# Large fp32 products as four column tiles, and a planner that knows the array's tilings

## The chip, the cores and the metric

The kernel runs on one core of one Trainium2 chip. The metric is the device time of one execution in microseconds (us), and lower is better. The core has five engines that work side by side and meet at semaphores: TensorE (PE, with its weight loads shown apart as PEld), VectorE (DVE), ScalarE (ACT), GpSimd (POOL) and SyncE (SP), which issues most of the transfers here.

## What is computed

Eight sequences of 512 tokens with 256 channels (x) pass through two layers; each has an attention part and a feed-forward part, and each part is added to x through a tanh gate. Everything is in fp32, apart from the quantised feed-forward products.

```python
x = x + tanh(g_xattn[0]) * L0_xattn(layernorm(x), ctx)   # 16 heads of 16: causal self + cross attention, one output projection
x = x + tanh(g_ffn[0])   * L0_ffn(layernorm(x))          # 8-bit affine quantised 256 -> 1024 -> gelu -> 256
x = x + tanh(g_xattn[1]) * L1_xattn(layernorm(x), ctx)   # two blocks, below
x = x + tanh(g_ffn[1])   * L1_ffn(layernorm(x))          # ternary weights 256 -> 1024, conv of 3 tokens, silu, -> 256

# one block of L1_xattn: 16 heads of 32, then an MLP; a1 attends to x, a2 to ctx (128 channels)
q, k, v = ln(x) @ wq, ln(y) @ wk, ln(y) @ wv
a = softmax(q @ k.T * 32 ** -0.5)        # in block a1 a strict mask follows the softmax
x_out = x + (a @ v) @ li1 + li1_b
out = x_out + gelu(ln(x_out) @ li2 + li2_b) @ li3 + li3_b    # 256 -> 1024 -> 256
```

## The kernel before

**Stages.** The work runs in four overlapping stages. By the trace, layer 0's attention lasts until about 713 us, layer 0's feed-forward part until about 1060 us, layer 1 with both its blocks and most of its feed-forward part until about 2600 us, and the rest is the end of the last sequences.

**Three tilings of the array.** The array of TensorE is used in three ways, which the trace shows in the form of each product:

- "rows" (`32*128`): the scores of attention, `ps_s<-QT,KT`. Four heads lie at partitions 0, 32, 64 and 96, and the four products of a set go to four row tiles (`front`, L1422 and L2206).
- "columns" (`128*32`): attention's product with the values, `ov<-pt,v`, `ov<-pt,vt` and `ov<-dg,vt`, and the sums of the exponentials, `ps<-acc,ones` and `ps<-pt,ones`. The four products of a set write to PSUM partitions 0, 32, 64 and 96 (`back`, L1441 and L2229).
- "whole" (`128*128`): all projections and MLP products in fp32 (`proj`, L1058, and direct calls of `mm`, L1052), the bf16 products of the feed-forward parts, the transposes (`tp`, L1056), and small products of 1 or 128 columns (`gains1`, `row_of`).

An fp32 product of any tiling appears in the trace as two MATMUL records and two LDWEIGHTS records; a bf16 product or a transpose as one of each. Nearly all go through `mm`, so the profile gives L1053 as their line, and they are told apart by their tiles: `ps<-x3T,li` and `ps<-li,hD` are the two MLP products of layer 1, `ps<-li,oT` its output projection, `ps<-zT,a_wq`, `ps<-zT,a_wk` and `ps<-a_wv,zT` its queries, keys and values; `xnT`, `ctxT` and `yT` belong to layer 0; `ps<-hp,diag` is a convolution done as products with diagonal matrices, in the tail of the last sequence only; `fw` and `f_w_q` are the bf16 weights of the feed-forward parts.

**Attention.** One step is a front and a back. A front writes four score products into two PSUM tiles (`ps_s`, tag `st`), and ACT takes their exponentials to `pt` (L1431, L2217); for masked blocks POOL clears part of it (L1434) or copies the masked diagonal to `dg` (L2221). The back multiplies with the values into `ov`, a PSUM tile of which there is one (tags `ov` and `ov1`). In layer 1, DVE adds the `pt` tiles of a group of four heads (`acc`, L2246 and L2248); the last back of a group forms the sums with `ones`, and then DVE turns them (`rt`, L2261), takes reciprocals, turns them back (`rb`, L2264) and multiplies them into `oT` (L2266), which frees `ov`. There are 64 groups in layer 1.

**What sets the order.** The order of instructions on every engine is fixed while the program is written. Two loops, `weave_timed` (L1067, layer 0) and `weave_all` (L1824, layer 1), choose again and again between the next step of attention and a number of generators ("streams") for projections, norms, the MLP and the feed-forward parts. A stream yields the tiles that its next piece needs. Of the pieces that could start by TensorE's planned time plus 0.3 us, the one with the lowest progress (base + share x work done / total) is written; if there is none, the one that can start first. `sooner` (L797) picks ACT or DVE for an evacuation by the planned times of both.

The planned times come from `Pace` (L756). Its `note` (L801) is called for every instruction and adds up when each engine is free (`free`), when each tile is ready (`done`) and last used (`used`), and how much work TensorE did (`work`). A tiled product is priced in `quarter` (L860), which keeps four lanes, one for each tile of the array; other products in `cost` (L874). A product's result counts as ready at the end of its streaming. `Pace.note` also ties each engine's instructions into the order in which they were written.

**Weights of the feed-forward parts.** `few_weights` (L1896) loads the bf16 weights of one feed-forward part from DRAM through SP (L1900) each time that a stream asks for them: `first(b)` (L1918) w2 of layer 0, `last(b)` (L2286) w1 and w2 of layer 1. The tiles `fw1` and `fw2` have one buffer each, and both layers use `fw2`. The streams run one after another: first 0 to 5, last 0, first 6, last 1, last 2, first 7, last 3 to 6. The tail of sequence 7 uses the weights that last 6 took.

Of the kernel before, what the change touches and what calls it, by code (L numbers as in the profile page):

```python
# [8 lines left out]
F32 = mybir.dt.float32  # L9
BF16 = mybir.dt.bfloat16  # L10
# [3 lines left out]
PSUM = bass.MemoryType.PSUM  # L14

P = 128
# [4 lines left out]
FF = 1024  # L21
# [7 lines left out]
FIRST_AT = (-1, 0, 1, 2, 4, 5, 7, 9)  # L29
LAST_AT = (6, 7, 8, 11, 12, 13, 15)  # L30
PTS = 3
KEYS_FIRST = 6


# [23 lines left out]
class General:  # L58
    def __init__(self, tc, ins, out):
        self.tc, self.nc, self.ins, self.out = tc, tc.nc, ins, out  # L60
# [695 lines left out]
class Pace:  # L756
# [2 lines left out]

    SIGNAL, OVERLAP = 0.04, 0.07

    def __init__(self, tc):
        self.tc, self.nc = tc, tc.nc
        self.free = {}
        self.done = {}
        self.used = {}
        self.rings = {}
        self.last = {}  # L770
        self.work = 0.0
        self.table = None
        self.wire = 0.0

        self.groups, self.lanes, self.start = None, [0.0] * 4, 0.0

    def open(self):
        self.nc.push_inst_callback(self.note)
# [22 lines left out]
    def note(self, ins):  # L801
        e = str(ins.engine).rsplit(".", 1)[-1]
        outs = [a.bass_ap for a in ins.outs if hasattr(a, "bass_ap")]
        srcs = [a.bass_ap for a in ins.ins if hasattr(a, "bass_ap")]
        if not outs or not srcs and ins.opcode != "Memset":
            return
        if e in self.last:
            self.tc.add_manual_dep(
                ins, self.last[e],
                mybir.DependencyInfo(mybir.DependencyClass.NoSync, mybir.DependencyReason.DATA),  # L810
                reason="woven order",
            )
        self.last[e] = ins.name
        out = self.name(outs[0])
        tiled = e == "PE" and 32 in tuple(ins.tile_size)
        t0 = 0.0 if tiled else self.free.get(e, 0.0)
        if out not in self.used:
            tile_ = outs[0].tensor
            bufs = getattr(tile_, "tag_meta", None) and tile_.tag_meta.bufs
            if bufs:  # L820
                tag = tile_.tag.rsplit("_", 2)[0]
                tiles, _, _ = ring = self.rings.get(tag, ([], 0, None))
                if ring[2] != tile_.owner_uid:
                    tiles, _, _ = self.rings[tag] = ([], bufs, tile_.owner_uid)
                if len(tiles) >= bufs:
                    t0 = max(t0, self.used[tiles[-bufs]] + self.SIGNAL)
                tiles.append(out)
        elif e != "PE" and ins.opcode != "DMACopy":
            t0 = max(t0, self.used[out] + self.SIGNAL)
        for a in srcs:  # L830
            t0 = max(t0, self.done.get(self.name(a), 0.0) + self.SIGNAL)
        if ins.opcode == "DMACopy":
            self.free[e] = t0 + 0.4
            n = 4 if outs[0].dtype == F32 else 2
            for _, k in outs[0].ap:
                n *= k
            self.wire = max(self.wire, t0 + 1.2) + n / 280e3
            end = self.wire + 1.2
        elif tiled:
            cost, end = self.quarter(ins, t0, outs)  # L840
        else:
            cost = self.cost(e, ins, outs, srcs)
            self.groups = None if e == "PE" else self.groups
            end = t0 + cost
            self.free[e] = end - (self.OVERLAP if e in ("DVE", "Activation") else 0.0)
            if e == "PE":
                self.work += cost
        self.done[out] = max(end, self.done.get(out, 0.0))
        for a in outs + srcs:
            n = self.name(a)  # L850
            self.used[n] = max(end, self.used.get(n, 0.0))
# [5 lines left out]
            n *= k  # L857
        return n

    def quarter(self, ins, t0, outs):  # L860

        rows = ins.tile_size[0] == 32
        if self.groups is not rows:
            self.groups, self.lanes = rows, [self.free.get("PE", 0.0)] * 4
        k = ins.tile_position[0 if rows else 1] // 32
        t = max(t0, self.lanes[k], self.start + 0.02)
        n = self.size(outs[0])
        cost = 0.19 + n * 0.0017 if rows else 0.1 + n * 0.00177
        self.start, self.lanes[k] = t, t + cost
        self.free["PE"] = max(self.lanes)  # L870
        self.work += cost / 4
        return cost / 4, t + cost

    def cost(self, e, ins, outs, srcs):  # L874
        size = self.size

        op = str(ins.opcode)
        n = max(size(a) for a in outs + (srcs if "Reduce" in op else []))

        few = sum(size(a) == 1 for a in srcs)  # L880
        if e == "PE":
            start = 0.0 if self.groups is None else 0.19
            if ins.is_transpose:
                return start + 0.095
            return start + max(0.22, n * 0.00169) if srcs[0].dtype == F32 else start + n * 0.00042
        if e == "Activation":
            f = str(getattr(ins, "func", "Copy")).rsplit(".", 1)[-1]
            sbuf = srcs[0].tensor.space != PSUM
            t = n * 0.00084 + 0.16
            if f == "Identity":  # L890
                t += 0.22 if sbuf else 0.09 * few
            elif f == "Gelu" and n <= T:
                t += 0.19
            if f in ("Exp", "Gelu", "Silu") and f != self.table:
                self.table = f
                t += 1.28
            return t
        psum = any(a.tensor.space == PSUM for a in outs + srcs)
        two = sum(size(a) == n for a in srcs) > 1
        if e == "Pool":  # L900
            if "Affine" in op:
                return 0.25 + n * 0.001
            return 1.05 if n <= 2 * NT and two else 0.22 + n * 0.0021
        if "Reduce" in op:
            return 0.14 + n * (0.00173 if len(srcs[0].ap) > 2 and list(srcs[0].ap)[-1][0] > 1 else 0.00106)
        if "BNStats" == op:
            return 0.41
        if n <= 4 * NT:
            return 0.17
        if psum or two or "Transpose" in op:  # L910
            return 0.15 + 0.05 * few + n * 0.00106
        return 0.15 + 0.05 * few + n * 0.0006
# [39 lines left out]
class Fast(General):  # L952
# [97 lines left out]


    def mm(self, out, lhsT, rhs, start=True, stop=True):  # L1052
        self.nc.tensor.matmul(out, lhsT, rhs, start=start, stop=stop, skip_group_check=True)  # L1053

    def tp(self, out, in_):
# [540 lines left out]
    def layer0_ffn(self):  # L1596
        nc, tc, small = self.nc, self.tc, self.small
        with (
# [15 lines left out]
            for b in range(B):  # L1614
                streams.append(Stream(self.range0(b), 4.7, 1.0, b))
            streams.append(Stream(self.chain(*(self.keys2(b) for b in range(KEYS_FIRST))), 64.0, B))
            self.weave_timed([], streams)
# [85 lines left out]
    def keys2(self, b):  # L1703

        work, w = self.work, self.w1s[1]
        cT = self.cTs.pop(0)
        if b + 2 < KEYS_FIRST:
            self.load_cT(b + 2)
# [5 lines left out]
    def keys2_rest(self):  # L1714
# [13 lines left out]

        load(KEYS_FIRST)
        load(KEYS_FIRST + 1)  # L1730
        for b in range(KEYS_FIRST, B):
            k = work.tile([P, 4, T], F32, tag="pt", name="k2", bufs=PTS)
            yield from self.keys_of(b, cTs[b], w[0], k)
            v = work.tile([P, NT, 2 * C], F32, tag="pt", name="v2", bufs=PTS)
            yield from self.values_of(b, cTs.pop(b), w[1], v)
# [31 lines left out]
    def layer1_xattn(self):  # L1767
        nc, tc = self.nc, self.tc
        with (
# [11 lines left out]
            self.hps = [wpool.tile([P, T // 2 + 3], F32, name=f"hp{i}") for i in range(2)]  # L1781
            for t in self.hps:
                nc.gpsimd.memset(t, 0.0)
            self.wl = {}


            self.pairs = self.fronts = self.backs = self.zTs = self.nvt = 0
# [26 lines left out]
            self.keys_done, self.x0_read = False, 0  # L1814
            keys = [Stream(self.keys2_rest(), 8.0 * (B - KEYS_FIRST), 1.0, -1.0)]
            self.weave_all(
# [79 lines left out]
    def few_weights(self, layer, names):  # L1896
        out = []
        for n in names:
            t = self.wst.tile([P, 2 * FF], BF16, tag=f"f{n}", name=f"f{n}")
            self.nc.sync.dma_start(t, self.fwd[f"f{layer}_{n}"])  # L1900
            out.append(t.rearrange("p (c f) -> p c f", c=2) if n == "w1" else t.rearrange("p (f c) -> p f c", f=NF))
        return out

# [14 lines left out]
    def first(self, b):  # L1918
# [4 lines left out]
        def load_h(half):  # L1923
            if b or not half:
                h = work.tile([P, NF, n], F32, tag="hF", name="hF")
            else:
                h = work.tile([P, NF, n], F32, tag="pt", name="hF", bufs=PTS)
            nc.sync.dma_start(
# [262 lines left out]
    def steps1(self, b, blk):  # L2191
# [14 lines left out]
        def front(g, n):  # L2206
# [5 lines left out]
            for j in (2, 3, 0, 1):  # L2212
                r = slice(32 * j, 32 * j + 32)
                self.mm(pss[j // 2][:, j % 2, :], KT[r, diag], QT[r, :])
            pt = work.tile([P, 4, T], F32, tag="pt", name="pt", bufs=PTS)
            for jp in (1, 0):
# [174 lines left out]
    def tail(self, half):  # L2391
# [35 lines left out]
        cols = slice(half * (n - 1), half * (n - 1) + n + 1)  # L2427
        h = work.tile([P, NF, n], F32, tag="pt", name="h7", bufs=PTS)
        for f in range(NF + 1):
# [172 lines left out]
```

## Time and profile before

| What | Value |
|---|---|
| Runs | 2786.3, 2784.82 and 2781.45 us, median 2784.82 |
| Span of the profiled execution | 2779.7 us, 38478 instructions |
| Mean granted TensorE clock | 0.959 of full speed |
| TensorE waits, 100 to 713 us | 15.9 us of 613 |
| TensorE waits, 713 to 1060 us | 70.1 us of 347 |
| TensorE waits, 1060 to 2600 us | 97 us of 1540 |
| fp32 products at `128*128`, 512 columns | 868 records |
| fp32 products at `128*128`, 256 columns | 2984 records |
| Transposes and fp32 products of 128 columns or fewer | 720 records |
| bf16 products | 891 records |

The profiled execution is one run of the program under the hardware profiler; durations are taken from it, and its span is 5.1 us under the median of the runs. The waits are sums over the view that tells who waited for whom. Matmul records overlap, since the ends of pipelined products are modelled: what a product costs the stream is read from the distance of the starts, not from the duration.

How lines are read. A line of the timeline has the start in us from the start of the span, the length from its first start to its last end, the engine, the line of the program, the operation, "out<-in" by the names of the tiles, the tiling and shape, and the number of records merged into it; in brackets at the end stands the idle time before it with what ended it. A line of waits has who waited, the instruction that ended the wait, total us, number and the longest one. A line of stretches has the window, its length, and for each engine the busy us with the number of instructions in brackets, then the granted clock, the share of DMA and GB/s.

### The profile page before, as it was taken

The page shows a single profiled execution, that of the slowest core. Times are in us where ns is not written, and L with a number is a line of the kernel's source. Part 1 is how long each engine was busy: PE and PEld are TensorE (multiplying, and loading weights), DVE is VectorE, ACT ScalarE, POOL GpSimd, SP SyncE. Part 2 cuts the span into 40 slices and gives each one's busy share as a digit, 9 for nine tenths or more (in the row PEclk, how much of TensorE's full clock was granted, in tenths as well). Part 3 has the DMA queues.
Part 4 walks back from the last instruction along what each step waited for, and adds up shares of the span by engine and source line. Part 5 has one row for each costly group of instructions (what it writes and reads, how often), then busy time and mean ns, then how long its engine had stood idle before and what let it go on. Part 6 is the DMA issues. An engine that isn't in the chain of part 4 may idle for free.

```text
span 2779.7 us, 38478 instructions
## 1 busy us (share of the span) xinstructions
PE 2517.8 (91%) x15447; PEld 1223.8 (44%) x15452; DVE 1736.5 (62%) x3135; ACT 1452.2 (52%) x1803; POOL 614.8 (22%) x682
## 2 busy tenths in 40 slices
PE   7999999999786989999999999988999989999875
PEld 2333333333233344535554535545455454454554
DVE  4544554343476666564666777676777877767766
ACT  4666666656573554445444455444554555555421
POOL 2212222111001344231334231111114332101100
PEclk9999999999886999999999999999999999999987
DMA  3001120000364512211211013211021102211010
GB/s 113 25 27 50 50 73 16 20 31 12 118 261 173 178 46 99 80 46 42 76 60 63 16 54 107 69 38 58 24 82 60 43 4 89 71 45 43 23 38 17
DMA packets 76475, 176.55 MB, mean 64 GB/s; under 512 B 7424, under 2 KB 36480, under 8 KB 68992
## 3 DMA queue, kind: packets, MB, share of 16 engines
q1 hardware_dynamic: 73904, 170.81, 17.6%
q8 instruction: 123, 2.02, 0.3%
q0 software_dynamic: 800, 2.62, 0.3%
q10 hardware_dynamic: 1584, 0.58, 0.1%
q14 instruction: 64, 0.52, 0.1%
HBM read 111.07 MB, written 62.91 MB: 63 GB/s over the span
## 4 chain that ended last, share of the span: by engine, by line
PE 46%; DVE 13%; ACT 4%; POOL 2%; issue 2%; DMA 0%; ACTq 0%; POOLq 0%; DVEq 0%; SPq 0%
PE ps L1053 31%; PE ps_s L1053 8%; PE ov L1053 6%; ACT pt L2217 2%; PE ps L1056 1%; DVE hF L2332 1%; DVE acc L2246 1%; POOL dg L2221 1%; DVE rb L2264 1%; DVE hm L2342 1%; DVE z L144 1%; DVE mv L1971 1%; DVE rt L2261 1%; DVE oT L2266 1%; DVE acc L2248 1%
## 5 line engine op out<-in xcount | busy, mean ns | idle before, releaser
L2217 ACT ACTIVATE pt<-ps_s 128x1024 f32<-128x1024 f32 x512 | 496.3, 1021 | 418.0 <-PE ps_s L1053 313.6
L1053 PE MATMUL ps_s<-QT,KT 32*128 32x512 f32 (+3 forms) x4096 | 613.2, 607 | 28.3 <-ACT pt L2217 16.1
L1431 ACT ACTIVATE pt<-ps_s 128x1024 f32<-128x1024 f32 (+3 forms) x512 | 411.2, 862 | 202.6 <-PE ps_s L1053 194.3
L1053 PEld LDWEIGHTS ps_s<-QT,KT 32*128 32x128 f32 x4096 | 191.6, 184 | 368.0 <-issue 201.8
L1053 PE MATMUL ps<-x3T,li 128*128 128x256 f32 x1024 | 244.9, 391 | 3.9 <-DVE hp L2320 2.4
L1053 PE MATMUL ov<-pt,v 128*32 128x512 f32 (+3 forms) x2048 | 232.7, 525 | 13.5 <-POOL pt L1434 12.7
L1053 PE MATMUL ps<-li,hD 128*128 128x256 f32 x1024 | 239.1, 389 | 5.7 <-ACT hD L2164 5.7
L1053 PE MATMUL ov<-pt,vt 128*32 128x512 f32 (+3 forms) x1792 | 204.4, 526 | 36.2 <-DVE oT L2266 29.4
L1977 POOL TENSOR_SCALAR mv<-mv 128x2 f32<-128x2 f32 (+1 forms) x105 | 57.7, 550 | 770.4 <-DVE mv L1972 735.3
L2221 POOL TENSOR_SCALAR_AFFINE_SELECT dg<-pt 128x512 f32<-128x512 f32 x128 | 116.1, 908 | 505.6 <-ACT pt L2217 505.4
L1053 PEld LDWEIGHTS ps<-x3T,li 128*128 128x128 f32 x1024 | 192.5, 194 | 60.7 <-issue 18.4
L1053 PEld LDWEIGHTS ps<-li,hD 128*128 128x128 f32 x1024 | 193.8, 194 | 56.4 <-issue 14.5
L1434 POOL TENSOR_SCALAR_AFFINE_SELECT pt<-pt 128x512 f32<-128x512 f32 x128 | 86.3, 674 | 471.7 <-ACT pt L1431 470.0
L2248 DVE TENSOR_TENSOR acc<-acc,pt 128x2048 f32<-128x2048 f32 x64 | 149.4, 2334 | 4.3 <-ACT pt L2217 3.2
L2246 DVE TENSOR_TENSOR acc<-pt 128x2048 f32<-128x2048 f32 x64 | 149.2, 2332 | 1.1 <-ACT pt L2217 1.1
L1456 DVE STREAM_TRANSPOSE ot<-ov 128x512 f32<-128x512 f32 x64 | 45.8, 716 | 165.9 <-PE ov L1053 165.9
L2332 DVE SCALAR_TENSOR_TENSOR hF<-hp,cols,hF 128x256 f32<-128x256 f32 x224 | 114.6, 512 | 41.7 <-ACT hF L2323 35.6
L1053 PE MATMUL ps<-zT,a_wq 128*128 128x512 f32 x256 | 127.8, 623 | 2.1 <-DVE zT L2058 2.1
L1053 PE MATMUL ps<-li,oT 128*128 128x256 f32 x512 | 128.0, 394 | 1.7 <-DVE oT L2266 1.0
L1759 ACT ACTIVATE hD<-ps,cols 128x256 f32<-128x256 f32 x123 | 54.7, 471 | 137.1 <-PE ps L1053 100.5
L1053 PEld LDWEIGHTS ov<-pt,v 128*32 128x32 f32 x2048 | 40.4, 108 | 167.1 <-issue 100.2
L1053 PEld LDWEIGHTS ps<-li,oT 128*128 128x128 f32 x512 | 92.9, 191 | 47.7 <-issue 16.1
(305 smaller groups left out, 3654.9 us busy)
## 6 DMA issues: line engine op xcount, KB each, us to landing
hd<-h SPq DMA_DIRECT2D x16, 1024.0 KB, 3.9
hF<-hd SPq DMA_DIRECT2D x16, 1024.0 KB, 6.7
li<-in_w_a_dram SPq DMA_DIRECT2D x12, 1024.0 KB, 5.0
fw<-q_f_w SPq DMA_DIRECT2D x22, 512.0 KB, 5.5
xF<-xd SPq DMA_DIRECT2D x22, 512.0 KB, 5.1
kd<-k SPq DMA_DIRECT2D x8, 1024.0 KB, 3.9
vd<-v SPq DMA_DIRECT2D x8, 1024.0 KB, 5.2
res<-rd SPq DMA_DIRECT2D x32, 256.0 KB, 2.8
```

The lines of the kernel that those rows point to most:

```text
L144: self.nc.vector.tensor_scalar(out[:, i, :], x[:, i, :], mv[:, i, 0:1], rstd[:, i : i + 1], ALU.subtract, ALU.mult,)
L1053: self.nc.tensor.matmul(out, lhsT, rhs, start=start, stop=stop, skip_group_check=True)
L1431: nc.scalar.activation(pt[:, 2 * jp : 2 * jp + 2, lo:], pss[jp][:, :, lo:], AF.Exp)
L1434: nc.gpsimd.affine_select(out=diag, in_=diag, compare_op=ALU.is_ge, fill=0.0, base=0, pattern=[[0, 4], [1, P]], channel_multiplier=-1,)
L1456: nc.vector.transpose(ot.rearrange("p b d -> p (b d)"), ov)
L1759: self.nc.scalar.activation(out, ps, AF.Identity, bias=bias)
L1977: nc.gpsimd.tensor_scalar(rstd, mv[:, :, 1], EPS, None, ALU.add)
L2217: nc.scalar.activation(pt[:, 2 * jp : 2 * jp + 2, :], pss[jp], AF.Exp)
L2221: nc.gpsimd.affine_select(out=dg, in_=pt[:, :, diag], compare_op=ALU.is_gt, fill=0.0, base=0, pattern=[[0, 4], [-1, P]], channel_multiplier=1,
L2246: nc.vector.tensor_tensor(st["acc"], st["pt"], pt, ALU.add)
L2248: nc.vector.tensor_tensor(st["acc"], st["acc"], pt, ALU.add)
L2332: nc.vector.scalar_tensor_tensor(a, hp[:, half + k : half + k + n], self.col("conv_w", 3 * f + k), a, ALU.mult, ALU.add)
```

## The change

It has four parts.

1. `mm` splits a product whose stationary operand is fp32 and 128 x 128, and whose result has 256 columns or more, into four products of 32 stationary columns each, which write to PSUM partitions 0, 32, 64 and 96. The 128-column fp32 products, the transposes and the bf16 products stay as they are.
2. `Pace` prices all of TensorE's products in one function, `array`, in place of `quarter` and the PE part of `cost`. It has three modes. Leaving a mode costs a fixed time (`LEAVE`), streaming costs 0.001667 us a column in fp32 and 0.000417 in bf16 plus 0.005, a transpose 0.108, and a result is ready 0.17 us (`DRAIN`) after the end of its streaming.
3. ACT's reading of a PSUM tile is planned to begin no sooner than 0.1 us (`TO_ACT`) after the tile is ready.
4. `few_weights` keeps the tile that it loaded last and loads again only when the layer is another one.

The loops that choose, the streams, their shares and totals, and the number of buffers are unchanged.

```diff
+COLS = True
...
-    SIGNAL, OVERLAP = 0.04, 0.07
+    SIGNAL, OVERLAP, DRAIN, TO_ACT = 0.04, 0.07, 0.17, 0.1
+    LEAVE = {"rows": 0.21, "columns": 0.13, "whole": 0.195}
...
-        tiled = e == "PE" and 32 in tuple(ins.tile_size)
-        t0 = 0.0 if tiled else self.free.get(e, 0.0)
+        t0 = 0.0 if e == "PE" else self.free.get(e, 0.0)
...
-        elif tiled:
-            cost, end = self.quarter(ins, t0, outs)
+        elif e == "PE":
+            end = self.array(ins, t0, outs, srcs[0].dtype == F32)
         else:
             cost = self.cost(e, ins, outs, srcs)
-            self.groups = None if e == "PE" else self.groups
+            if e == "Activation" and srcs[0].tensor.space == PSUM:
+                t0 = max(t0, self.done[self.name(srcs[0])] + self.TO_ACT)
             end = t0 + cost
...
-    def quarter(self, ins, t0, outs):
-
-        rows = ins.tile_size[0] == 32
-        if self.groups is not rows:
-            self.groups, self.lanes = rows, [self.free.get("PE", 0.0)] * 4
-        k = ins.tile_position[0 if rows else 1] // 32
-        t = max(t0, self.lanes[k], self.start + 0.02)
-        n = self.size(outs[0])
-        cost = 0.19 + n * 0.0017 if rows else 0.1 + n * 0.00177
-        self.start, self.lanes[k] = t, t + cost
+    def array(self, ins, t0, outs, f32):
+
+        rows, columns = ins.tile_size[0] == 32, ins.tile_size[1] == 32
+        mode = "rows" if rows else "columns" if columns else "whole"
+        if mode != self.mode:
+            end = self.free.get("PE", 0.0) + self.LEAVE.get(self.mode, 0.0)
+            self.mode, self.lanes, self.start = mode, [end] * 4, end
+        k = ins.tile_position[0 if rows else 1] // 32 if rows or columns else 0
+        t = max(t0, self.lanes[k], self.start)
+        if ins.is_transpose:
+            cost = 0.108
+        else:
+            cost = self.size(outs[0]) * (0.001667 if f32 else 0.000417) + 0.005
+        self.start = t
+        if mode == "whole":
+            self.lanes = [t + cost] * 4
+        else:
+            self.lanes[k] = t + cost
         self.free["PE"] = max(self.lanes)
-        self.work += cost / 4
-        return cost / 4, t + cost
+        self.work += cost if mode == "whole" else cost / 4
+        return t + cost + self.DRAIN
...
-        if e == "PE":
-            start = 0.0 if self.groups is None else 0.19
-            if ins.is_transpose:
-                return start + 0.095
-            return start + max(0.22, n * 0.00169) if srcs[0].dtype == F32 else start + n * 0.00042
...
     def mm(self, out, lhsT, rhs, start=True, stop=True):
+        if lhsT.dtype == F32 and tuple(lhsT.shape) == (P, P) and out.shape[-1] >= 2 * P and COLS:
+            for j in range(0, P, 32):
+                self.nc.tensor.matmul(
+                    out[j : j + 32], lhsT[:, j : j + 32], rhs, start=start, stop=stop, skip_group_check=True
+                )
+            return
         self.nc.tensor.matmul(out, lhsT, rhs, start=start, stop=stop, skip_group_check=True)
...
         for n in names:
-            t = self.wst.tile([P, 2 * FF], BF16, tag=f"f{n}", name=f"f{n}")
-            self.nc.sync.dma_start(t, self.fwd[f"f{layer}_{n}"])
+            if self.few_now.get(n, (None,))[0] != layer:
+                t = self.wst.tile([P, 2 * FF], BF16, tag=f"f{n}", name=f"f{n}")
+                self.nc.sync.dma_start(t, self.fwd[f"f{layer}_{n}"])
+                self.few_now[n] = (layer, t)
+            t = self.few_now[n][1]
```

More of the change, by code (lines that the diff above doesn't have):

```diff
@@ L773, in __init__ @@
         self.wire = 0.0
-        self.groups, self.lanes, self.start = None, [0.0] * 4, 0.0
+        self.mode, self.lanes, self.start = None, [0.0] * 4, 0.0
     def open(self):
@@ L838, in note @@
             end = self.wire + 1.2
-        elif tiled:
-            cost, end = self.quarter(ins, t0, outs)
+        elif e == "PE":
+            end = self.array(ins, t0, outs, srcs[0].dtype == F32)
         else:
             cost = self.cost(e, ins, outs, srcs)
-            self.groups = None if e == "PE" else self.groups
+            if e == "Activation" and srcs[0].tensor.space == PSUM:
+                t0 = max(t0, self.done[self.name(srcs[0])] + self.TO_ACT)
             end = t0 + cost
             self.free[e] = end - (self.OVERLAP if e in ("DVE", "Activation") else 0.0)
-            if e == "PE":
-                self.work += cost
         self.done[out] = max(end, self.done.get(out, 0.0))
@@ L880, in cost @@
         few = sum(size(a) == 1 for a in srcs)
-        if e == "PE":
-            start = 0.0 if self.groups is None else 0.19
-            if ins.is_transpose:
-                return start + 0.095
-            return start + max(0.22, n * 0.00169) if srcs[0].dtype == F32 else start + n * 0.00042
         if e == "Activation":
@@ L1783, in layer1_xattn @@
                 nc.gpsimd.memset(t, 0.0)
-            self.wl = {}
+            self.wl, self.few_now = {}, {}
             self.pairs = self.fronts = self.backs = self.zTs = self.nvt = 0
```

## The prediction

> **What bounds the kernel now.** I read the page first: its busy shares, the strip of granted clock and the chain of work that ended last.
>
> ```profile
> PE 2517.8 (91%) x15447; PEld 1223.8 (44%) x15452; DVE 1736.5 (62%) x3135; ACT 1452.2 (52%) x1803; POOL 614.8 (22%) x682
> ...
> PEclk9999999999886999999999999999999999999987
> ...
> PE ps L1053 31%; PE ps_s L1053 8%; PE ov L1053 6%; ACT pt L2217 2%; PE ps L1056 1%; DVE hF L2332 1%; DVE acc L2246 1%; POOL dg L2221 1%; DVE rb L2264 1%; DVE hm L2342 1%; DVE z L144 1%; DVE mv L1971 1%; DVE rt L2261 1%; DVE oT L2266 1%; DVE
> ```
>
> TensorE is busy 91% of the span and carries the chain; the group to be changed (ps, 31%) is its largest part. Next, the stretches by engine, because an average hides stages:
>
> ```profile
> 100.00:713.00 613.00, 595.36 (x4224) 211.68 (x4216) 280.32 (x591) 399.58 (x505) 118.70 (x162) 1.00 0.10 34
> 713.00:1060.00 347.00, 276.51 (x1366) 136.66 (x1370) 218.06 (x311) 180.69 (x245) 72.66 (x78) 0.88 0.41 156
> 1060.00:2600.00 1540.00, 1442.56 (x8833) 759.97 (x8831) 1073.55 (x1849) 771.87 (x909) 389.71 (x396) 0.97 0.17 58
> 2600.00:2780.00 180.00, 121.79 (x556) 85.15 (x548) 123.21 (x250) 50.74 (x81) 11.63 (x19) 0.81 0.07 24
> ```
>
> After the length come PE, PEld, DVE, ACT and POOL, the granted clock and DMA. Layer 0 attention (to 713 us) is TensorE at 97%. The layer-0 FFN (713 to 1060) and the tail (from 2600) are not bound by it: 80% and 68%, at a lower clock. In layer 1 (1060 to 2600) TensorE has 94% and DVE 70%. What TensorE waits for there:
>
> ```profile
> PE ov L1053 <- DVE oT L2266: 26.5, 16, 4.9
> PE ps_s L1053 <- ACT pt L2217: 15.7, 24, 2.4
> PE ps L1056 <- DVE z L144: 14.9, 16, 3.0
> ```
>
> All its waits there come to some 97 us of 1540, none above 27.
>
> Last, what a change of tiling costs, from the start times of neighbours:
>
> ```profile
> 1046.81 3.72 PE L1053 MATMUL ps<-li,hD 128*128 128x256 f32 x16
> 1050.46 1.14 PE L1053 MATMUL ps_s<-QT,KT 32*128 32x512 f32 x8
> 1051.53 1.98 PE L1053 MATMUL ps<-zT,a_wk 128*128 128x512 f32 x4
> 1053.44 0.64 PE L1053 MATMUL ov<-pt,vt 128*32 128x256 f32 x8
> 1053.90 0.40 PE L1053 MATMUL ov<-dg,vt 128*32 128x128 f32 x8
> 1054.23 3.72 PE L1053 MATMUL ps<-li,hD 128*128 128x256 f32 x16
> 1057.88 1.14 PE L1053 MATMUL ps_s<-QT,KT 32*128 32x512 f32 x8
> ...
> 1504.19 1.04 PE L1053 MATMUL ps<-acc,ones 128*32 128x512 f32 x8
> 1505.05 1.04 PE L1053 MATMUL ps<-pt,ones 128*32 128x512 f32 x8
> ```
>
> An fp32 product is two records. Inside a whole run records start 0.2158 us apart for 256 columns and 0.429 for 512. So 16 of them need 3.453, yet the next product starts 3.65 after the first: a whole run costs 0.198 over its streaming (about 0.104 on entry, 0.094 on leaving). The rows take 1.07 for 0.858 of streaming: 0.21. Columns: 0.46+0.33 for 0.432+0.218: 0.139 (0.024 on entry, 0.115 on leaving). Two column sets in a row start 0.86 apart: four tiles of 512 columns stream as fast as one whole product of 512, and a set after a set pays nothing.
>
> [...]
>
> **The change, part by part.**
>
> 1. Splitting in `mm`. 3852 records (868 of 512 columns, 2984 of 256), that is 1926 products, become four column tiles each: 11,556 more matmuls and as many weight loads. Streaming: nothing, as the sets above show. Weight loads: a whole one takes 194 ns, a 32-column one 109, and the dg set (eight loads, 0.218 us of streaming) hides them; nothing. What changes is the runs. I counted runs of one tiling over the matmuls of the trace in order, then again with those 3852 called columns, and priced each run at 0.21 (rows), 0.139 (columns), 0.198 (whole):
> - 0 to 713: whole 133 to 29, columns 252 to 257, rows 254 both: 114.7 to 94.8 us, -19.9.
> - 713 to 1060: 76 runs to 118, since projections now alternate with bf16 products and transposes that stay whole: +6.5.
> - 1060 to 2600: whole 294 to 166, columns 230 to 284, rows 230 both: 138.5 to 120.6, -17.9.
> - 2600 to the end: 10 to 56 (the diagonal products of the tail alternate with bf16 ones): +7.7.
>
> In the seven products above (1051.53 to 1057.88, 6.35 us) it would leave 5.96: two whole runs and one column run become one column run, less 2 x 0.198.
>
> What of it reaches the end: in layer 0 nearly all, for between 100 and 713 TensorE waits 16 us in all; I take -19. In layer 1 a faster TensorE runs into DVE's chain in places; I take four fifths, -14 (bounds -8 and -18). In the FFN stage TensorE waits some 70 us of 350, partly hiding the switches: +4 (0 to +7[...]). In the tail TensorE is busy 68% and mostly waits for DVE (hp, hm, hq), which hides part of them: +4 (0 to +8). Sum -25.
>
> 2. The account. It now charges the drain of each tiling, 0.17 us until a product is readable and 0.1 more for ACT. Nothing in the instructions changes but their order, on all engines and on SP's queue, whose loads are written in the same weaving. The old account charged a column set 0.1+0.00177n, 1.006 us at 512, where 0.858 is seen inside a run, and let ACT read at the last column. So it thought TensorE slow and results early; both let it write a product ahead of its operand. The waits on pt, dg and KT that such misjudgement makes are some 50 us over the kernel. I take -5; bounds: -25 if half go, +45 if the new order meets the accumulator's wait (below). The choice between ACT and DVE for evacuation tilts to DVE by at most the 0.1.
>
> 3. `few_weights` keeps the tile while the layer is the same. In the order of the streams (first of 0 to 5, last 0, first 6, last 1 and 2, first 7, the rest) w2 is loaded 6 times for 15 and w1 once for 7: 15 of 22 DMAs go, 7.9 of 176.55 MB.
>
> ```profile
> fw<-q_f_w SPq DMA_DIRECT2D x22, 512.0 KB, 5.5
> q8 instruction: 123, 2.02, 0.3%
> ```
>
> No wait of TensorE names their landing, and the DMA engines are 17% busy in layer 1; taken as nothing (0 to -2). SP's queue has 15 fewer entries that could hold others up.
>
> 4. More instructions. Some 31,000 of PE are fetched in 123 packets; 23,112 more are about 90 packets. [...] "issue" ends only 9.6 us of TensorE's waits now: nothing. At worst each packet's time (0.3% of 16 engines' 2779.7 us over 123, 1.08 us) stood on the path: +97.
>
> Sum: -30 against the profiled execution, 2779.7 to about 2750. Its median lies 5.1 above that span; I carry the difference over: 2784.8-30 = 2755.
>
> **The rivals.**
>
> - B, swallowed in layer 1: the merged runs only lengthen TensorE's waits for DVE, -19+8 with nothing from the rest: 2774. For it: DVE at 70%. Against: none of the waits is large, and TensorE is busy for 94% of the stage.
> - C, the account pays more: the order fits the chip, and a third of layer 1's 97 us of waits goes, some -30 in place of -5: 2730.
> - D, slower, through the accumulator: `ov1` has one buffer, and the first back of a group waits for DVE's rt, rec, rb, oT. 64 groups share these 29.4 us of waits now, 0.46 each. If the new order puts other DVE work ahead of that chain so that each group waits 0.8 longer, +51: 2806. It decides from 0.47 a group (30/64). For it: the longest wait is already 4.9 us, and the order is re-made everywhere with the streams' shares left as they were. Against: the new account lets DVE start later after a product, as it does.
> - E, instructions starve TensorE: +97-30 gives 2852; decides from 0.33 us a packet. Against: dg sets pass 16 instructions in 0.24 us now.
> - F, the change doesn't do what it says: the new order breaks runs as often as it joins them (about 1480 runs again): 2784.
>
> **How the numbers follow.** Chances: forecast 0.56, B 0.14, C 0.13, D 0.11, E 0.02, F 0.04. No change means within 0.2%, 5.6 us, about what a measurement of this kernel can tell. Faster takes the forecast, C and most of B: 0.79. Same: F and a little of B and D, 0.08. Slower: 0.13. The likeliest's own range is 2738 to 2772 (the bounds of layer 1 and of the account's small gains); with half of C and all of B, 8 in 10 lie in 2730 to 2786.
>
> **What would show it.** Right: only bf16 products and 128-column ones remain at 128*128; rows of li, zT and oT become 128*32 with four times the count; a set of 256 columns starts 0.432 after the last; runs of one tiling near 1390; layer 0's attention ends near 694 us, not 713; the weights of the few load 7 times. Wrong: sets of 256 spaced well over 0.45 (instructions or loads), a longer wait of ov on oT, or TensorE's waits in layer 1 clearly above 97 us. The forecast fails first if the new order, which I can't see, moves layer 1 by more than the switches.

## The result, and the profile after

The changed kernel takes 2795.3 us (median of 4 runs, 2793.3 to 2799.8) against 2783.1 for the kernel before: a ratio of 1.0046, 95% interval 1.0032 to 1.0060. It is slower by some 12 us, where 30 us less had been forecast. The profiled execution has a span of 2798.0 us, 18.3 above that of before.

The busy shares and the granted clock on the page of the changed kernel:

```profile
PE 2497.6 (89%) x27008; PEld 994.1 (36%) x27008; DVE 1739.5 (62%) x3143; ACT 1453.7 (52%) x1795; POOL 605.2 (22%) x682
...
PEclk9999999999887999999999999999997999999976
```

TensorE has 27,008 matmuls for 15,447 and is busy 20 us less, although the span is longer: the added time is idle time. The clock shows a 7 in a slice late in layer 1 (2098 to 2168 us), where there was a 9.

The stretches that were read before the change, now with the end moved to 2798:

```profile
100.00:713.00 613.00, 585.62 (x5612) 189.82 (x5612) 284.36 (x598) 404.87 (x503) 118.78 (x165) 0.99 0.10 36
713.00:1060.00 347.00, 276.04 (x2530) 108.33 (x2525) 222.64 (x309) 175.85 (x235) 70.36 (x79) 0.89 0.40 151
1060.00:2600.00 1540.00, 1437.77 (x16858) 606.00 (x16854) 1056.45 (x1827) 774.09 (x917) 382.47 (x393) 0.97 0.17 55
2600.00:2798.00 198.00, 117.45 (x1274) 63.74 (x1262) 132.17 (x271) 48.44 (x74) 11.64 (x19) 0.76 0.05 17
```

Nothing in layer 1 stands out at this width. TensorE's waits there, the three longest:

```profile
PE ps_s L1062 <- ACT pt L2229: 16.1, 29, 1.6
PE ps L1062 <- DVE hq L1963: 12.4, 2, 12.0
PE ov L1062 <- POOL dg L2233: 11.2, 9, 3.8
```

All its waits there sum to 101 us, hardly more than the 97 of before, and the wait of `ov` for `oT` has fallen from 26.5 to 9.9. But one wait for `hq`, the rounded input of a feed-forward product, lasts 12.0 us. Around it, in one narrow stretch, much time is lost. First before, then after the change:

```profile
2080.00:2300.00 220.00, 200.76 (x1301) 112.81 (x1300) 168.22 (x307) 112.03 (x136) 79.78 (x83) 0.98 0.13 45
```

```profile
2080.00:2300.00 220.00, 177.23 (x1980) 77.46 (x1982) 147.34 (x275) 90.91 (x108) 67.70 (x68) 0.88 0.15 49
```

TensorE is busy 24 us less in it, and its clock falls from 0.98 to 0.88. TensorE's timeline at the hole:

```profile
2145.60 1.94 PE L1062 MATMUL ps<-acc,ones 128*32 128x512 f32 x8
2147.30 1.92 PE L1062 MATMUL ps<-pt,ones 128*32 128x512 f32 x8
2149.16 1.92 PE L1062 MATMUL ps<-fw,hq 128*128 128x256 bf16 x16
2163.04 1.04 PE L1062 MATMUL ps<-fw,hq 128*128 128x256 bf16 x4 [11.96 <-DVE hq L1963]
2164.49 2.74 PE L1062 MATMUL ps<-fw,hq 128*128 128x256 bf16 x12 [0.42 <-DVE hq L1963]
2167.03 1.91 PE L1065 MATMUL ps<-ident,z 128*128 128x128 f32 x8
2171.22 0.34 PE L1065 MATMUL ps<-ident,xP 128*128 128x128 f32 x1 [2.28 <-ACT xP L1995]
```

The sums of the last back of sequence 6 (`acc,ones`, `pt,ones`) are written, and no other attention follows. TensorE has only the product of `first(7)` to do (`fw,hq`), the piece that gives sequence 7 its input. SP's queue shows why it comes so late, before and then after:

```profile
2076.53 0.53 SPq L1928 DMA_DIRECT2D hF<-hd  x1
2098.80 0.53 SPq L1928 DMA_DIRECT2D hF<-hd  x1
```

```profile
2116.64 0.53 SPq L1940 DMA_DIRECT2D hF<-hd  x1
2153.09 0.53 SPq L1940 DMA_DIRECT2D hF<-hd  x1
```

These are the two loads with which `first(7)` begins its halves. They come 40 and 54 us later than before, while attention up to sequence 6 ends 53 us sooner (last `oT` of sequence 6's first block at 2151 for 2204). The pause to the next `oT`, the first of sequence 7, is 94 us in place of 25, before and then after:

```profile
2203.98 0.69 DVE L2266 TENSOR_TENSOR oT<-ov,rb 128x512 f32<-128x512 f32 x1
2229.40 0.69 DVE L2266 TENSOR_TENSOR oT<-ov,rb 128x512 f32<-128x512 f32 x1
```

```profile
2151.09 0.69 DVE L2278 TENSOR_TENSOR oT<-ov,rb 128x512 f32<-128x512 f32 x1
2244.81 0.69 DVE L2278 TENSOR_TENSOR oT<-ov,rb 128x512 f32<-128x512 f32 x1
```

The end got longer too. The last stores of the outputs show it; a store from `xF` is a `last(b)`, one from `res` a half of the tail. Before, then after:

```profile
2654.28 0.39 SPq L2373 DMA_DIRECT2D out_dram<-xF  x1
2744.69 0.39 SPq L2470 DMA_DIRECT2D out_dram<-res  x1
2764.76 0.39 SPq L2373 DMA_DIRECT2D out_dram<-xF  x1
2775.04 0.37 SPq L2470 DMA_DIRECT2D out_dram<-res  x1
```

```profile
2684.02 0.39 SPq L2385 DMA_DIRECT2D out_dram<-xF  x1
2721.16 27.92 SPq L2482 DMA_DIRECT2D out_dram<-res  x2
2791.65 0.37 SPq L2385 DMA_DIRECT2D out_dram<-xF  x1
```

Before, the feed-forward chain's last piece, `last(6)`, ended between the two halves of the tail. Now both halves are out by 2749 and `last(6)` ends alone, at 2792. From the last `oT` to the end it takes 197 us in place of 164. The last `oT` itself comes at 2601 us for 2615, still some 15 us sooner than before: the hole eats a part of what was won, and the late end the rest and more.

So one thing is late in both places: the chain of feed-forward streams (`first` and `last`). The two theories that the experiments had to tell apart were: the columns pay as forecast, and the new order, made by the new account, holds that chain back (theory 1); or the columns cost something themselves (theory 2).

### The profile page after: what moved, and what is told of

It is laid out like the page before. It is cut to its first block, busy times and chain, and to the rows that moved or that the text cites. A ratio compares the mean times of both kernels' runs of the same rounds, so it can differ in the third digit from the quotient of the medians.

```text
span 2798.0 us, 61637 instructions
## 1 busy us (share of the span) xinstructions
PE 2497.6 (89%) x27008; PEld 994.1 (36%) x27008; DVE 1739.5 (62%) x3143; ACT 1453.7 (52%) x1795; POOL 605.2 (22%) x682
## 4 chain that ended last, share of the span: by engine, by line
PE 45%; DVE 13%; ACT 5%; POOL 2%; issue 2%; DMA 0%; ACTq 0%; POOLq 0%; DVEq 0%
PE ps L1058 23%; PE ps_s L1062 8%; PE ps L1062 7%; PE ov L1062 5%; ACT pt L2229 2%; DVE acc L2258 1%; PE ps L1065 1%; DVE hF L2344 1%; DVE mv L1983 1%; POOL dg L2233 1%; DVE hm L2354 1%; DVE rb L2276 1%; DVE rt L2273 1%; DVE z L145 1%; DVE oT L2278 1%
## 5 line engine op out<-in xcount | busy, mean ns | idle before, releaser
L2229 ACT ACTIVATE pt<-ps_s 128x1024 f32<-128x1024 f32 x512 | 496.2, 1021 | 414.6 <-PE ps_s L1062 292.9
L1058 PE MATMUL ps<-li,hD 128*32 128x256 f32 x4096 | 238.7, 388 | 9.5 <-ACT hD L2176 9.5
L2233 POOL TENSOR_SCALAR_AFFINE_SELECT dg<-pt 128x512 f32<-128x512 f32 x128 | 123.0, 961 | 560.4 <-ACT pt L2229 560.3
L1058 PE MATMUL ps<-x3T,li 128*32 128x256 f32 x4096 | 240.4, 386 | 1.8 <-DVE x3T L2154 1.6
L1062 PE MATMUL ov<-pt,vt 128*32 128x512 f32 (+3 forms) x1792 | 198.8, 513 | 17.9 <-DVE oT L2278 13.6
L1989 POOL TENSOR_SCALAR mv<-mv 128x2 f32<-128x2 f32 (+1 forms) x105 | 49.1, 468 | 723.3 <-DVE mv L1984 694.6
L1058 PEld LDWEIGHTS ps<-li,hD 128*32 128x32 f32 x4096 | 131.7, 112 | 119.3 <-issue 24.5
L1058 PEld LDWEIGHTS ps<-x3T,li 128*32 128x32 f32 x4096 | 128.6, 111 | 107.9 <-issue 23.5
L1058 PE MATMUL ps<-zT,a_wq 128*32 128x512 f32 x1024 | 125.7, 609 | 0.8 <-DVE zT L2070 0.8
L1058 PE MATMUL ps<-li,oT 128*32 128x256 f32 x2048 | 122.5, 380 | 2.4 <-DVE oT L2278 2.1
L1062 PE MATMUL ps<-fw,hq 128*128 128x256 bf16 x512 | 76.2, 310 | 42.0 <-DVE hq L1963 25.4
L1770 DVE TENSOR_SCALAR hD<-ps,cols 128x256 f32<-128x256 f32 x143 | 65.6, 480 | 73.5 <-PE ps L1058 56.4
```

The costliest lines, as they stand in the source:

```text
L1058: self.nc.tensor.matmul(out[j : j + 32], lhsT[:, j : j + 32], rhs, start=start, stop=stop, skip_group_check=True)
L1770: self.nc.vector.tensor_scalar(out, ps, bias, None, ALU.add)
L1989: nc.gpsimd.tensor_scalar(rstd, mv[:, :, 1], EPS, None, ALU.add)
L2229: nc.scalar.activation(pt[:, 2 * jp : 2 * jp + 2, :], pss[jp], AF.Exp)
L2233: nc.gpsimd.affine_select(out=dg, in_=pt[:, :, diag], compare_op=ALU.is_gt, fill=0.0, base=0, pattern=[[0, 4], [-1, P]], channel_multiplier=1,
```

## The experiments

The table has for each kernel the number of fronts of layer 1 (of the 192 ahead of sequence 7's attention) that had begun when `first(7)` loaded its first half, the pause between the last `oT` ahead of sequence 7 and its first one, and the time from the last `oT` of all to the end, all three read off the trace, and the median with the ratio to the kernel before on the same chip.

| Kernel | Fronts begun | Pause, us | End, us | Median, us | Ratio (95%) |
|---|---|---|---|---|---|
| before | 176 | 25 | 164 | 2781.8 to 2784.8 | 1 |
| after the change | 187 | 94 | 197 | 2795.3 | 1.0046 (1.0032 to 1.0060) |
| e1 order kept, split | 176 | 24 | 166 | 2759.3 | 0.9921 (0.9906 to 0.9935) |
| e2 old account, split | 172 | 26 | 161 | 2765.5 | 0.9939 (0.9926 to 0.9953) |
| e3 new account, no split | 192 | 108 | 187 | 2846.0 | 1.0230 (1.0214 to 1.0246) |
| e4 first(7) at 7.5 | 164 | 18 | 199 | 2776.7 | 0.9980 (0.9972 to 0.9988) |
| e5 slack 1.25 | 171 | 23 | 158 | 2772.4 | 0.9964 (0.9950 to 0.9979) |
| e6 slack 1.5 | 171 | 24 | 160 | 2778.7 | 0.9989 (0.9980 to 0.9997) |
| e7 no drain | 184 | 87 | 176 | 2782.2 | 0.9999 (0.9989 to 1.0008) |
| e8 loads back | 192 | 105 | 175 | 2809.2 | 1.0097 (1.0080 to 1.0114) |
| e9 split where it joins | 176 | 25 | 169 | 2757.5 | 0.9911 (0.9895 to 0.9926) |
| e10 and weights kept | 176 | 25 | 166 | 2755.9 | 0.9910 (0.9894 to 0.9927) |
| e11 old account, slack 0.65 | 192 | 119 | 172 | 2804.4 | 1.0070 (1.0057 to 1.0083) |
| e12 old account, slack 0.75 | 179 | 63 | 174 | 2777.7 | 0.9969 (0.9956 to 0.9982) |

### The columns alone, in the old order

The split is made, but the planner prices the first of the four products as the whole one and passes over the other three, so all that it decides stays as before.

```diff
     def note(self, ins):
...
         self.last[e] = ins.name
+        if self.part:
+            return
         out = self.name(outs[0])
-        tiled = e == "PE" and 32 in tuple(ins.tile_size)
+        tiled = e == "PE" and 32 in tuple(ins.tile_size) and self.part is None
...
     def mm(self, out, lhsT, rhs, start=True, stop=True):
+        if lhsT.dtype == F32 and tuple(lhsT.shape) == (P, P) and out.shape[-1] >= 2 * P:
+            for j in range(0, P, 32):
+                self.pace.part = j
+                self.nc.tensor.matmul(
+                    out[j : j + 32], lhsT[:, j : j + 32], rhs, start=start, stop=stop, skip_group_check=True
+                )
+            self.pace.part = None
+            return
```

> The kernel before, its order of instructions kept to the letter, with the large fp32 products split into four column tiles and nothing else of the change. Theory 1 (the columns pay, the new order loses): all four tiles stream as one whole product and the runs fall from 1479 to 1394, so the time falls by 15 to 24 us, to 2759 to 2768. Theory 2 (the columns themselves cost, through 23,000 more instructions and weight loads): no gain or a loss, 2783 or more.

It took 2759.3 us: 23 us less than before, as the forecast for the columns said (24 by the count of runs). Its timeline shows the price of a set:

```profile
1010.18 1.91 PE L1059 MATMUL ps<-x3T,li 128*32 128x256 f32 x32
1012.02 1.14 PE L1064 MATMUL ps_s<-QT,KT 32*128 32x512 f32 x8
1013.09 7.11 PE L1059 MATMUL ps<-x3T,li 128*32 128x256 f32 x128
...
1024.15 1.90 PE L1059 MATMUL ps<-zT,a_wq 128*32 128x512 f32 x16
1025.87 0.40 PE L1064 MATMUL ov<-dg,vt 128*32 128x128 f32 x8
1026.09 1.04 PE L1064 MATMUL ps<-acc,ones 128*32 128x512 f32 x8
```

Four sets of 256 columns and the leaving take 1.84 us: 4 x 0.432 + 0.11. Two sets of 512, the former whole products, take 1.72, 2 x 0.86, and pass into the next column set without a pause. In the trace 1394 runs of one tiling are left (1393 changes), as many as the count had said. Theory 2 falls.

### The two accounts

Three kernels part the split from the account: the split planned by the old account, which makes a new order; the new account without the split (`COLS = False`, the weights kept as well); and the change with its two latencies at zero.

```diff
-    SIGNAL, OVERLAP, DRAIN, TO_ACT = 0.04, 0.07, 0.17, 0.1
+    SIGNAL, OVERLAP, DRAIN, TO_ACT = 0.04, 0.07, 0.0, 0.0
```

> The split with the old account, which prices a column set 0.1 + 0.00177 us a column; no other part of the change. The order is made anew, and in it first(7) starts 19 fronts ahead of sequence 7's attention (15 before the change, 5 after it). Theory 1: no hole in layer 1 before sequence 7, so a gain of 10 to 24 us, 2759 to 2773. Theory 2: 2795 as after the change.

> After the change, but nothing is split: the new account and the kept weights alone. In its order first(7) starts only with the first front of sequence 7's attention. Theory 1: a hole of TensorE of 40 to 70 us at 2150 to 2300, and none of the columns' gain: 2800 to 2840. Theory 2 (the columns cost): as before the change or better, 2775 to 2785.

> After the change, with the planned time until a product is readable (DRAIN) and ACT's extra (TO_ACT) set to zero; the prices of the tilings stay. In its order first(7) starts 8 fronts ahead. If those two terms alone hold the feed-forward chain back: 2755 to 2770. If the prices of the tilings do it as well: between, 2775 to 2792.

With the old account the new order is good: 2765.5. With the new account and nothing split the kernel loses 63 us and has the longest hole but one. So the account makes the loss, and the columns' gain hid a good part of it. The cleanest pair is `e2` and `e8` (below), the change with the loads of the weights put back: both split, both load at every call, and they differ in the account alone. It costs 44 us (2809.2 for 2765.5, and 44 by the ratios too). Without the latencies 13 us come back, of the 36 that lie between the change and the kept order; the rest of the account does its part. What part each single price has was not tried further.

### The feed-forward chain

In `e4` one number of the changed kernel is another: `FIRST_AT` ends with 7.5 in place of 9. In `e5` and `e6` it is the slack (`lag`) of the streams `first` and `last`: `weave_all` lets them write only when DVE's planned free time (for a few steps ACT's) less this slack has come.

```diff
-FIRST_AT = (-1, 0, 1, 2, 4, 5, 7, 9)
+FIRST_AT = (-1, 0, 1, 2, 4, 5, 7, 7.5)
```

```diff
-                few.append(Stream(self.first(b), 3.8, 0.8, k, 1.0))
+                few.append(Stream(self.first(b), 3.8, 0.8, k, 1.25))
...
-                few.append(Stream(self.last(b), 10.5, 0.8, k, 1.0))
+                few.append(Stream(self.last(b), 10.5, 0.8, k, 1.25))
```

> After the change, with one number changed: the place of first(7) in its chain of streams is 7.5 in place of 9, so that it comes before last(2). Theory 1: the hole before sequence 7's attention goes, 30 to 45 us: 2750 to 2768. Theory 2: the order of this stream doesn't matter, 2790 to 2798. Theory 3 (the end of the kernel is what got longer, since the chain of feed-forward streams is late as a whole): part of it only, 2775 to 2788.

> After the change, with the slack that a feed-forward stream has against DVE's planned time raised from 1.0 to 1.25 us. In its order first(7) starts 21 fronts ahead of sequence 7's attention (5 after the change, 15 before). Theory 1, now put more closely (the new account sets DVE's planned times further behind TensorE's, and the slack of 1.0 then holds the feed-forward chain back against attention): hole and late end both go, 2745 to 2762. Theory 2 (the new account orders badly for another reason, such as the choice between ACT and DVE): 2780 or more.

> As the run with 1.25, but with a slack of 1.5 us; first(7) again starts 21 fronts ahead. Theory 1: 2745 to 2765. Theory 2: 2780 or more.

With `first(7)` sooner the pause is 18 us and 19 us are won, but the end stays at 199: the third theory of that expectation. With a slack of 1.25 both are mended, and 23 us are won. The sizes were missed: 2772.4 and 2778.7 lie above the 2745 to 2765 of theory 1 and below the 2780 of theory 2. In those two orders attention itself runs later (last `oT` at 2615 and 2618, for 2590 in the kept order). A part of that is lost early. Layer 0's attention ends at 705 us in the kept order, after the change and with 1.25, but in the stretch that follows TensorE is busy 287 us in the kept order and 276 after the change, and a slack of 1.25 (277) doesn't alter it. First the kept order, then a slack of 1.25:

```profile
713.00:1060.00 347.00, 286.97 (x2644) 113.44 (x2644) 224.75 (x322) 182.43 (x247) 80.09 (x84) 0.89 0.42 156
```

```profile
713.00:1060.00 347.00, 276.52 (x2492) 107.73 (x2488) 220.90 (x305) 175.96 (x235) 69.76 (x77) 0.88 0.40 151
```

What in the new order loses it there is open. Each cure gives back only a part of the loss.

To see whether the slack alone makes the hole, I changed it in the other direction, with the old account. The split products are planned as whole ones, as in the first run, but the order is made anew:

> The split with the old account (split products planned as whole ones, as in the first run), with one number changed: the slack of the feed-forward streams against DVE's planned time is 0.65 in place of 1.0. The order is made anew, and first(7) starts only with the first front of sequence 7's attention. Theory 1 (a feed-forward chain held back by that slack makes the hole, whatever the account): a hole of TensorE of 40 to 70 us before sequence 7's attention, 2795 to 2825. Theory 2 (the new account's prices do harm in another way): no such loss with the old account, 2757 to 2770.

> The same with a slack of 0.75; first(7) starts 12 fronts ahead of sequence 7's attention. Theory 1: hardly any hole, 2757 to 2775. Theory 2: 2757 to 2770 as well, so that only the pair with 0.65 tells them apart.

With 0.65 the hole is there, without the new account: 2804.4 us, a pause of 119. TensorE's timeline of that kernel has the same pattern as the changed one, products that wait long for the `hq` of a feed-forward stream and nothing between them:

```profile
2162.12 1.03 PE L1064 MATMUL ps<-fw,hq 128*128 128x256 bf16 x4 [11.37 <-DVE hq L1962]
2165.60 2.74 PE L1064 MATMUL ps<-fw,hq 128*128 128x256 bf16 x12 [2.44 <-DVE hq L1962]
2179.69 0.61 PE L1064 MATMUL ps<-fw,hq 128*128 128x256 bf16 x2 [11.35 <-DVE hq L1962]
```

With 0.75 the pause is 63 us and the time 2777.7, just above what was expected; I had taken 12 fronts for enough. Over all kernels the pause follows the fronts begun: 18 to 26 us up to 176, then 63 (179), 87 (184), 94 (187), 105 to 119 (192).

### The weights kept

`few_weights` loads each time again, in the changed kernel; the planner sees the loads.

> After the change, with few_weights as it was (a load at every call). The planner counts the loads, so the order is made anew, and first(7) starts only with sequence 7's attention. Theory 1 (the order decides): slower than after the change, 2800 to 2825. Rival (the kept weights matter by themselves, a transfer saved or a wait): slower only by what 15 loads cost, within 2 us of 2795, wherever first(7) stands.

It took 2809.2, 14 us more than the change, with `first(7)` starting at front 192. As the order changed too, this run says nothing of the loads themselves. The pair `e9` and `e10` does. Both keep the old order, leave layer 0's feed-forward stage and the tail's diagonal products whole, and differ in the 15 loads alone.

```diff
+            self.split = False
             self.weave_timed([], streams)
+            self.split = True
...
+                self.split = False
                 for k in range(3):
                     self.mm(
                         ps, self.diag[3 * (f - 1) + k], hp[:, half + k : half + k + n], k == 0, k == 2
                     )
+                self.split = True
```

> As the run with the order kept, but the products of layer 0's feed-forward stage and the diagonal products of the tail are left whole, where split ones alternate with bf16 products and transposes. By the prices of the tilings this saves up to 13 us of switches there (6.5 and 7.7 by the count), part of which lies under waits. Theory: 2749 to 2757, below 2759. Rival (the switches there are hidden by waits for DVE and DMA): 2758 to 2761.

> As the one before, with the weights kept as after the change, and the planner told that they were loaded as before, so that the order of all other instructions stays. Theory 1 (the 15 loads are hidden): the same within 3 us of it. Rival (the loads delay others on SP's queue or on the wire): 3 us or more faster.

2757.5 and 2755.9 us, with intervals of the ratio that overlap widely, and that also overlap the first run's. By the medians the loads are worth 1.6 us and leaving those products whole 1.8, neither clear of the noise, although the latter takes 80 changes of tiling out of the trace (1313 for 1393). The 2757.5 of `e9` lies between its two forecasts and doesn't decide between them. `e10` has the lowest median and is faster than both kernels: 26 us under before on its chip, 39 under the change.

## Why the prediction was wrong

- **Splitting in `mm`: right.** The kept order gives 23 us for a forecast of 25. By stages, from the traces of before and of the kept order: layer 0's attention (to its last `ov`) ends at 705 for 720 us, -15 where -19 was taken; from there to layer 1's first front 204 us for 201, +3 where +4 was taken (201 again in `e9`, which leaves that stage's products whole); from there to the last `oT` 1680 for 1694, -14 as taken; the end 166 for 164, +2 where +4 was taken.
- **No cost of streaming, loads or instructions: right.** The sets stand as above; weight loads are busy 994 us in place of 1224. The packets of instructions went from 123 to 214, and rival E doesn't show. Rivals B and F fall too: layer 1 keeps its 14 us in the kept order, and the changed kernel has 1393 runs of one tiling, not 1480.
- **The account: wrong, and this is the step that failed.** It was taken at -5 us, with +45 as the far bound for the accumulator. The order that it makes costs +36 (2795.3 less the 2759.3 of the kept order, with the kept weights in the plan), +44 with the account alone changed (`e2` and `e8`), +63 without the split. The bound's size was near, its place was not: rival D looked at `ov` waiting for `oT`, which got shorter (29.4 to 13.6 us over the kernel). What went wrong was the order of whole streams: `first(7)` began when 187 of 192 fronts had begun, and `last(6)` was left over at the end. Two of its prices are near the trace of before: a column set of 512 columns is planned at 0.859 us (1.006 in the old account), where two in a row start 0.86 apart (1504.19 and 1505.05); and a result at 0.17 us after its streaming, where DVE's `rt` starts at 1506.16, 0.25 after the streaming of that second set (to 1505.91, by two records of 0.43).
- **Why I missed it.** I priced the account by the short waits that a wrong plan makes, and saw none of the kernel's order as a resource. The old order had its feed-forward chain 16 fronts ahead of need; the page before can't show such a margin, since nothing waits while it lasts. I named a fact close to the one that decides ("the streams' shares left as they were"), but only in support of D, and it is their slack, not their share, that the runs show at work. The prediction's last sentence said where it would fail first, a new order that moves layer 1; the sum gave that -5.
- **`few_weights`: right in size by itself** (1.6 us by the medians, not clear of the noise), but its loads are in the plan, so even this edit moves the order, by 14 us in the changed kernel.
- **The mark set for "wrong" was too blunt.** Layer 1's waits are 101 us for 97, 108 in the kept order, which is fast. Over 1540 us the hole drowned: TensorE's waits in 2080 to 2300 rose from 18 to 43 us, and the clock fell to 0.88.

How the new account holds the chain back is shown in the main. The runs show that a smaller slack makes the hole under the old account and that a larger one mends it under the new. The plan itself shows that the new account works the same way as a smaller slack: it sets DVE's planned free time further behind TensorE's, and that is the distance which the slack is held against. Read off `Pace` at each choice of `weave_all` up to the 192nd front, with the slack at 1.0, it is on average 1.60 us before the change and 1.43 in `e2`, but 1.75 after the change, 1.78 in `e8` and 1.64 without the latencies. Against `e2`, which is split as they are, that is 0.21 to 0.35 us more. A slack smaller by 0.25 and by 0.35 made a pause of 63 and 119 us under the old account, so the size fits. These are planned times; no run measures the distance on the chip. The choice between ACT and DVE hardly moved: in the changed kernel ACT has 8 instructions fewer in all, and DVE 8 more. One rival is left: the new account also books less work for the same products (the leaving isn't counted), and the streams' progress is reckoned from that. No run parts the two.

## What to carry to other kernels

Where a planner writes the order, its prices are a part of the schedule: a truer price can make a worse order if the weights and margins beside it were set with the old one. Part the two before judging either: run the new instructions in the old order, and the new order with the old instructions. And look for margins, not only for waits: how far ahead of its first use each chain of work runs is read from when it starts, not from who waits.

## What I had not expected of the hardware

More was lost around the hole than idle time. In 2080 to 2300 us TensorE's waits rise by 25 us, and the mean granted clock is 0.88 in place of 0.98. Just ahead of the longest wait, from 2145.6 to 2149 us, it is 0.50, and the two sums with `ones` start 1.70 us apart (2145.60 and 2147.30). In the same kernel, from 1021 to 1024 us, where the clock is 1.00, they start 0.86 apart (1021.44 and 1022.30). Over 2080 to 2300 us the clock is 0.98, 0.98 and 0.95 in three kernels with a short pause (`e1`, `e4` and `e5`), and 0.89, 0.90 and 0.86 in three with a long one (`e7`, `e8` and `e11`). That the waits bring the lower clock is not shown by this.

And a split product is as cheap in long runs as in short ones. In the kept order 16 sets (128 records) take 7.11 us from first start to last end, 0.44 a set with the end of the last one in it, and four sets with their leaving take 1.84, 0.46 a set; the page of the changed kernel has a weight load for each of these products (4096 loads for the 4096 records of `ps<-x3T,li`).
